# Attention inside a four-layer kernel: where VectorE makes its weight factors, when the last weight loads are asked for, and where the biases are added

## The chip, the cores and the metric

The kernel runs on one core of one Trainium2 chip. The time is device time in microseconds from launch to end, given as the median over runs. A profiled execution is a separate one; its span runs from its first to its last instruction.

## The reference, cut to what matters

Four layers run one after the other, each with a residual: `x = x + ffn(cond(x))`, with x of 8 x 128 tokens by 512. The change lies in the attention of the third layer and at the seam to what follows it:

```python
q = rope(rmsnorm(x @ Wq.T))          # 32 heads of 128
k = rope(rmsnorm(x @ Wk.T))          # 8 heads
v = x @ Wv.T
kc, vc = k_cache[block_table], v_cache[block_table]      # 512 cached rows for each of 8 sequences
scores = q @ concat(kc, k).T * SCALE                     # 640 keys, cached ones beyond the length hidden
probs = softmax(scores)
o = probs @ concat(vc, v)
y = o @ Wo.T
# next, the feed-forward of the same layer:
x = x + (y @ W.T + b) + delta(y)
```

All arithmetic is in float32.

## The kernel before

**Steps.** Attention is cut into 32 steps: `steps[n] = (qd, p)`, with `qd` one of 8 head groups (one key head and its four query heads) and `p` one of 4 pairs of sequences, so n = 4 qd + p. Within a step everything is done for both sequences j = 0, 1 of the pair.

**Seven products instead of eight.** The projection (`project`) and the output product (`leave`) multiply 2x2 block matrices with seven block products (`seven`, line 954). That needs sums of blocks on both sides. On the weight side they are the four *factors* (`blocks`, lines 866 to 879): `t1 = b12 - b11`, `t2 = b22 - t1`, `t3 = b22 - b12`, `t4 = b21 - t2`, each one VectorE subtraction, written `q_s<-q` or `q_s<-q,q_s` in the profile for the projection (128x768) and `o_s` for the output (128x512). `factors()` is a Python generator: every `next` issues one of them, so they can be placed one by one. `some(ops, k)` returns a function that issues the next k, `every(ops)` issues all that are left. On the token side the four sums are `xs` or `xs_all` (`tokens(n)`, for group 0, once for groups 1 to 6 together (for steps 4 to 7), and again for group 7) and `os` (`outputs`).

A `seven` runs on TensorE in the order one, six (t2), five (t1), six (t3), one, five (b22), six (t4). The arguments `at` name points between these at which other work is issued: `"u2"` after the second addition of the running sums `u`, `"c22"` after the additions that read the third product, and so on. The additions after a product (`put`, line 1017) write q, k and the new rows of `vals`. The last product (t4) is added into the same PSUM bank that the additions of c22 read, so TensorE can't start it before they are done.

**A step, in the order of the program.** `weigh(n, 0)`: scores of the first sequence on TensorE (`st`), exponentials on ScalarE (`pT`). `added(n, 0)`: four VectorE additions over the five blocks of keys (`part`), the first of which needs two blocks of `pT`, the second two more. `divided(n - 1)`: the previous step's `av` times the reciprocal sums `R`, two VectorE products into `oT`. `outputs(n - 1)`: the four token-side sums of `oT`. `project(n + 1)`. `rotate`, then, where a new head group begins at n + 2, the three loads of its weights (`weights`), and the POOL gathers of cached keys (`kn`). `leave(n - 1)`, whose last running sums POOL adds to y (lines 1218 and 1223). `turn` and `fetch` send queries and keys through DRAM to transpose them. Then `weigh(n, 1)` with `mix(n, 0)` (`av`) inside, `added(n, 1)`, `summed(n, 0)` and `summed(n, 1)` (a transpose `partT` and a reduction `rows`), `inverted(n)`, `mix(n, 1)`, `turn_cached(n + 2)` (two transposes `kt<-kn`, which need the gathered rows), and `tokens(n + 2)`.

**The way of the sums.** `inverted` copies the rows of three partition groups on ScalarE (line 1168), reduces, inverts and transposes on VectorE (`inv`, lines 1170 to 1172), and sends 4 KB to DRAM (`sums<-inv`, line 1175) and back to all partitions (`R<-sums`, 512 KB, line 1176). Both are on SP's queue, and the second waits there for the first.

**Order.** Nearly all of this is issued through `kept`, which keeps the order of the program on each engine's queue. Each engine works through its queue in order and waits on semaphores. What follows attention (`ending`) is partly left to a planner: its matmuls `h`, for one, have no fixed place.

**What the change moves.** In the kernel before, a new group's four projection factors are issued as follows, with n = 2, 6, ..., 26: two in step n between `added(n, 1)` and `summed(n, 1)`, one in step n + 1 after the first addition of `added`, one at `"u2"` of the next projection. The output factors of group 0 are issued in step 1: three at `"c22"` of `project`, one at `"c22"` of `leave`. `load_w2` and `load_aw` (lines 1757 to 1763) ask SP's queue for two weights of 1 MB each, `WT` and `AwT`, in step 30 before `mix`. `shifted` (line 1797) adds the biases of the feed-forward to x with four ScalarE activations, in step 31 after `weigh(31, 1)`.

Of the kernel before, what the change touches and what calls it, by code (L numbers as in the profile page):

```python
# [791 lines left out]
def attention(tc, a, x, ident, lens, kvrow, part, ww, wop, ypool, sums, rot, eps, psa, c2, chunks, mm):  # L792
# [52 lines left out]
    steps = [(qd, p) for qd in range(NQ) for p in range(NP)]  # L845
# [11 lines left out]
    def kept(i):  # L857
        return tc.keep_in_program_order(i) if running or i.ins.engine == pool.engine else i
# [38 lines left out]
    def every(ops):  # L897
        for _ in ops:
            pass
# [246 lines left out]
    def added(n, j):  # L1146

        t, u = (wk.tile([P, REP * P], F32, tag=f"part{k}{j * (k == 0)}", name=f"part{k}_{n}_{j}", bufs=1) for k in range(2))
        c = [S[n]["pT", j][:, k, :, :].rearrange("p i t -> p (i t)") for k in range(NC)]
        S[n]["part", j] = t  # L1150
        for o, l, r in ((t, c[0], c[1]), (u, c[2], c[3]), (t, t, u), (t, t, c[4])):
            kept(dve.tensor_tensor(o, l, r, ALU.add))  # L1152
            yield
# [8 lines left out]
        kept(dve.transpose(t, s["part", j].rearrange("p (b d) -> p b d", d=32)))  # L1162
        kept(dve.tensor_reduce(s["rows"][:, 0, j, :], t, AX.X, ALU.add))  # L1163

    def inverted(n):
        rows = S[n]["rows"].rearrange("p g j b -> p g (j b)")
        for g in range(1, 4):
            kept(act.copy(rows[0:32, g, :], rows[32 * g : 32 * g + 32, 0, :]))  # L1168
        r = wk.tile([32, 2, 32], F32, tag="inv", name=f"inv_{n}", bufs=1)
        kept(dve.tensor_reduce(r[:, 0, :], rows[0:32].rearrange("p g c -> p c g"), AX.X, ALU.add))  # L1170
        kept(dve.reciprocal(r[:, 0, :], r[:, 0, :]))
        kept(dve.transpose(r[:, 1, :], r[:, 0, :]))
        S[n]["R"] = R = wk.tile([P, 2, REP, P], F32, tag="R", name=f"R_{n}", bufs=1)
        here = sums[2 * n : 2 * n + 2, :].rearrange("j c -> (j c)")
        kept(sp.dma_start(here.rearrange("(c a) -> c a", a=32), r[:, 1, :]))
        kept(sp.dma_start(R.rearrange("p j i t -> p (j i t)"), here.partition_broadcast(P)))
# [102 lines left out]
    def run(pool_, end_of, bank, keep):  # L1279
        late.append(pool_)  # L1280
        y2 = ypool.tile([P, NB, D], F32, tag="y", name="y2")
        Y.append(y2)
        pool.memset(y2, 0.0)

        idle = psa.tile([P, 512], F32, tag="mm", name="idle_q", bufs=3)
        for _ in range(3):
            kept(pe.matmul(idle, x[:, 0, 0:P], x[:, 0, 0:512], start=True, stop=True))
        for j in range(2):
            squares(1, "q", j, range(REP))
            squares(1, "k", j, (0,))  # L1290
        keys_terms = rotate(1)
        read_cached = turn_cached(1, "xs")
        keys_terms()
        gather(1, "v")
        roots(1)
        rotated(1)
        normed(1)
        turn(1)
        end, prepared = None, iter(())
        w_ops, wo_ops = iter(()), WO[0].factors()  # L1300

        def some(ops, k=1):
            return lambda: [next(ops, None) for _ in range(k)]

        for n, (qd, p) in enumerate(steps):

            after = n + 1 if 0 < n < len(steps) - 1 else None
            weigh(n, 0)
            sums_of, outs = added(n, 0), iter(())
            next(sums_of)  # L1310
            some(w_ops)()
            every(sums_of)
            if n:
                divided(n - 1)
                outs = outputs(n - 1)
                if not after:
                    every(outs)
            if after:
                project(after, {
                    "u2": lambda: (every(outs), every(w_ops)),  # L1320
                    "c22": lambda: (turn_cached(2)() if n == 1 else None, some(wo_ops, 3)()),
                    "c11": lambda: (squares(after, "k", 0, (0,)), squares(after, "q", 0, (0, 1))),
                    "c12": lambda: squares(after, "q", 0, (2, 3)),
                })
                keys_terms = rotate(after)
                if n + 2 < len(steps):
                    if steps[n + 2][1] == 0:
                        weights(steps[n + 2][0])
                    gather(n + 2, "k")
                leave(n - 1, {  # L1330
                    "one": lambda: (
                        squares(after, "q", 1, range(REP)), squares(after, "k", 1, (0,)), roots(after),
                    ),
                    "c22": lambda: (every(wo_ops), keys_terms(), rotated(after), normed(after), turn(after)),
                })
                fetch(after)
                gather(after, "v")
            if n + 2 == len(steps):
                end.load_w2()
                end.load_aw()  # L1340
            mixed = mix(n, 0)
            left = (lambda: leave(n - 1),) if n and not after else ()
            weigh(n, 1, {2: (some(mixed), *left), 3: (some(mixed),), 4: (some(mixed, NC),)})
            if left:
                end.shifted()
            sums_of = added(n, 1)
            next(sums_of)
            summed(n, 0)
            if n == 0:
                next(sums_of)  # L1350
                fetch(1, read_cached)
                gather(2, "k")
            every(sums_of)
            if 0 < n < len(steps) - 2 and steps[n + 2][1] == 0:
                w_ops = W[steps[n + 2][0]].factors()
                some(w_ops, 2)()
            summed(n, 1)
            inverted(n)
            if n == 0:
                every(tokens(2))  # L1360
            if n == 5:
                prepared = end.prepare(bank, lambda shape, name: wk.tile(shape, F32, tag="xs", name=name, bufs=1))
            next(prepared, None)
            every(mix(n, 1))
            next(prepared, None)
            if n and p == 0:
                out_weights(qd)
                wo_ops = WO[qd].factors()
            if 0 < n < len(steps) - 2:
                turn_cached(n + 2)()  # L1370
                every(tokens(n + 2))
            if n == 3:
                kept(keep())
            if n == 4:
                end = end_of(kept)

            if qd == NQ - 1 and p:
                for j in range(2):
                    end.turn(y2, 2 * (p - 1) + j, bank)
            if n + 2 == len(steps):  # L1380
                end.low(0, bank)
                end.anchors(0, bank)
        divided(n)
        every(outputs(n))
        end.product(0, "st", bank)
        leave(n)
        return y2, end
# [903 lines left out]
```

## Time and profile before

| what | value |
|---|---|
| median of 3 runs | 1513.34 us (1511.30 to 1516.49) |
| the profiled execution | 1513.29 us, of which its span 1511.4 us |
| mean granted TensorE clock | 0.998 |
| busy: PE / VectorE (DVE) / ScalarE (ACT) / POOL | 1483.4 / 1079.4 / 565.6 / 847.7 us |
| matmuls st (L1132, cached and new keys) / av (L1183) | 301.5 / 290.6 us |
| DMA | 174.05 MB, mean 115 GB/s |

The page lists busy time of each engine and the costliest groups of instructions. The view of waits says, for each engine, whom it waited for: total, number, and longest. The timeline lists one engine's instructions: start, duration, engine, line, operation, output and inputs, count, and in brackets the idle time before it with the one that ended it. The chain of waits goes back from the last instruction to what released each step; "issue" is time in which an engine waited for nothing that the profile shows. Attention's steps lie between 328 and 1372 us of the span.

### The profile page before, as it was taken

Reading aid. Unit: us, or ns where it says so; the run is one execution under the profiler, and the core shown is the slowest. Engines: PE = TensorE matmul, PEld = TensorE weight load, DVE = VectorE, ACT = ScalarE, POOL = GpSimd, SP = SyncE. Lnnn points to the kernel's source line nnn. Section 1 sums busy time; section 2 is a strip of 40 time slices with the busy share of each in tenths; the row PEclk is TensorE's granted clock in tenths of the full one; section 3 lists DMA queues with packets and bytes.
Section 4 is the critical chain, followed back from the end, with each engine's and each line's share of the span. In section 5 each row is a group of like instructions: output and inputs, shape, how many; then the busy total and the mean of one; then the engine's idle time right before and its main releaser. Section 6 shows DMA issues by size and latency. Waiting matters only on the chain.

```text
span 1511.4 us, 18134 instructions
## 1 busy us (share of the span) xinstructions
PE 1483.4 (98%) x5615; PEld 939.9 (62%) x5615; DVE 1079.4 (71%) x2121; ACT 565.6 (37%) x1432; POOL 847.7 (56%) x869
## 2 busy tenths in 40 slices
PE   8999999999999999999999999999999999999998
PEld 7888787445555655555555555555555555559886
DVE  4566524388888787887778778778877888855375
ACT  1111101054444544454554444455445445431110
POOL 2232103476776777776677767677777767621210
PEclk9999999999999999999999999999999999999999
DMA  7411001144556434554444455445445544432001
GB/s 238 117 43 32 1 1 54 52 117 134 160 140 204 142 114 129 154 159 147 134 148 116 132 147 175 127 133 152 127 128 161 159 117 135 116 106 96 1 7 53
DMA packets 159306, 174.05 MB, mean 115 GB/s; under 512 B 54753, under 2 KB 129697, under 8 KB 159073
## 3 DMA queue, kind: packets, MB, share of 16 engines
q1 hardware_dynamic: 140768, 135.47, 30.8%
q0 software_dynamic: 17056, 36.49, 7.8%
q10 hardware_dynamic: 1376, 0.85, 0.2%
q8 instruction: 47, 0.77, 0.2%
q14 instruction: 59, 0.48, 0.1%
HBM read 130.66 MB, written 42.07 MB: 114 GB/s over the span
## 4 chain that ended last, share of the span: by engine, by line
PE 78%; DVE 12%; DMA 5%; issue 2%; ACT 1%; POOL 0%; SPq 0%; DVEq 0%; ACTq 0%
PE st L1132 14%; PE av L1183 13%; PE g L362 8%; PE q_six L968 7%; PE wo_two L968 5%; PE dn L362 5%; PE q_one L968 4%; PE q_five L968 4%; PE wo_one L968 3%; PE wo_six L968 3%; PE eo_l L53 2%; DVE q_s L875 2%; PE h L1719 2%; PE z L1719 2%; DMA R<-sums 2%
## 5 line engine op out<-in xcount | busy, mean ns | idle before, releaser
L911 POOL DMA_INDIRECT kn<-in_k_cache,kvrow_k x256 | 273.9, 1070 | 73.3 <-issue 69.8
L911 POOL DMA_INDIRECT vals<-in_v_cache,kvrow_v x256 | 272.7, 1065 | 73.5 <-issue 50.5
L1183 PE MATMUL av<-pT,vals 128*128 128x512 f32 x640 | 290.6, 592 | 1.5 <-DVE oT L1193 1.5
L1136 ACT ACTIVATE pT<-st,hide 128x512 f32<-128x512 f32 x256 | 176.0, 687 | 167.5 <-PE st L1132 167.2
L1132 PE MATMUL st<-qT,kT 128*128 128x512 f32 x512 | 236.1, 594 | 2.0 <-DMA qT<-turned_new 1.9
L1183 PEld LDWEIGHTS av<-pT,vals 128*128 128x128 f32 x640 | 121.4, 190 | 154.4 <-issue 147.3
L1057 POOL TENSOR_TENSOR vq<-q,txq 128x256 f32<-128x256 f32 x128 | 120.0, 966 | 150.5 <-DVE q L1017 78.5
L1132 PEld LDWEIGHTS st<-qT,kT 128*128 128x128 f32 x512 | 96.3, 190 | 111.8 <-issue 105.6
L1152 DVE TENSOR_TENSOR part<-pT 128x512 f32<-128x512 f32 x128 | 88.0, 688 | 71.8 <-ACT pT L1136 68.5
L968 PE MATMUL q_one<-q,x 128*128 128x384 f32 x256 | 93.0, 486 | 0.0
L1041 ACT ACTIVATE sqq<-q 128x128 f32<-128x128 f32 x256 | 79.4, 310 | 20.8 <-DVE q L1017 14.2
L968 PEld LDWEIGHTS q_one<-q,x 128*128 128x128 f32 x256 | 48.5, 190 | 39.8 <-issue 13.6
L968 PE MATMUL q_six<-q_s,xs_all 128*128 128x384 f32 x192 | 69.8, 486 | 0.0
L1022 ACT COPY q<-q_one 128x256 f32<-128x256 f32 x32 | 11.9, 373 | 148.7 <-PE q_one L968 148.7
L968 PE MATMUL wo_one<-o,oT 128*128 128x256 f32 x256 | 65.8, 379 | 0.2 <-DVE oT L1193 0.2
L1132 PE MATMUL st<-qT,kTn 128*128 128x512 f32 x128 | 65.4, 592 | 0.0
L1168 ACT COPY rows<-rows 32x32 f32<-32x32 f32 x96 | 20.7, 216 | 115.5 <-DVE rows L1163 114.7
L968 PE MATMUL wo_two<-o_s,os 128*128 128x256 f32 x256 | 60.6, 380 | 0.4 <-DVE vals L1017 0.4
L1136 ACT ACTIVATE pT<-st,rs 128x512 f32<-128x512 f32 x64 | 44.0, 687 | 38.4 <-PE st L1132 38.4
L429 POOL TENSOR_TENSOR ws<-wu 128x256 f32<-128x256 f32 (+1 forms) x9 | 6.6, 734 | 92.1 <-DMA wu<-in_WuT 92.1
L968 PEld LDWEIGHTS wo_one<-o,oT 128*128 128x128 f32 x256 | 48.6, 190 | 13.8 <-issue 0.5
L968 PE MATMUL q_six<-q_s,x 128*128 128x384 f32 x128 | 47.2, 492 | 9.1 <-DVE vals L1017 9.1
(451 smaller groups left out, 2861.2 us busy)
## 6 DMA issues: line engine op xcount, KB each, us to landing
turned_new<-qkt SPq DMA_DIRECT2D x126, 160.0 KB
turned_cached<-kt SPq DMA_DIRECT2D x128, 128.0 KB
kT<-turned_cached SPq DMA_DIRECT2D x32, 512.0 KB
qT<-turned_new SPq DMA_DIRECT2D x32, 512.0 KB
R<-sums SPq DMA_DIRECT2D x32, 512.0 KB
q<-in_WqT SPq DMA_DIRECT2D x8, 1024.0 KB
o<-in_WoT SPq DMA_DIRECT2D x8, 1024.0 KB
kn<-in_k_cache,kvrow_k POOLq DMA_INDIRECT x256, 3.0
```

The source lines that it names most:

```text
L53: pe.matmul(o, lhsT, rhs, start=start, stop=stop)
L362: pe.matmul(o, lhsT, rhs, start=start, stop=stop, skip_group_check=True)
L875: kept(dve.tensor_tensor(o, l, r, ALU.subtract))
L911: kept(pool.indirect_dma_start(out=d[:, c, :], out_offset=None, in_=kc if what == "k" else vc, in_offset=bass.IndirectOffsetOnAxis(ap=kvro ...
L968: kept(pe.matmul(o, l[:, c, :], r[:, c, :], start=start and c == 0, stop=c == 1, skip_group_check=True))
L1041: kept(act.activation(sq, S[n][m][:, j, i, :], AF.Square, accum_out=S[n]["ssq"][:, j, col : col + 1]))
L1057: kept(pool.tensor_tensor(to, t[:, b, :, hi : hi + 64], wx[:, b, lo : lo + 64].unsqueeze(2).to_broadcast(list(to.shape)), ALU.mult,))
L1132: kept(pe.matmul(ps, s["kT"][:, c, 4 * j : 4 * j + 4, :] if c < 4 else s["kn"][:, j], s["qT"][:, :, REP * j : REP * (j + 1), :].rearrange( ...
L1136: kept(act.activation(pT[:, c, :, :].rearrange("p i t -> p (i t)"), ps, AF.Exp, **(dict(bias=hide[:, b, c : c + 1]) if c < 4 else dict(bia ...
L1152: kept(dve.tensor_tensor(o, l, r, ALU.add))
L1183: kept(pe.matmul(ps, v[:, c, :], pT[:, c, :, :].rearrange("p i t -> p (i t)"), start=c == 0, stop=c == NC - 1, skip_group_check=True,))
L1719: return pe.matmul(o, lhsT, rhs, start=start, stop=stop, skip_group_check=True)
```

## The change

It has four parts.

1. A new group's projection factors: the first is issued inside `inverted`, behind ScalarE's row copies and ahead of VectorE's reduction of them; the second after `turn_cached(n + 2)`; the third after the first addition of the next step, as before; the fourth after the last of these additions, ahead of `divided`.
2. The output factors of group 0, in step 1: two ahead of the first addition of `added(1, 0)`, one after it, one at `"c22"` of the projection.
3. `load_w2` and `load_aw`, in step 30, follow `inverted`, so they stand behind `sums` and `R` on SP's queue.
4. `shifted`, in step 31, follows `inverted`, so the four activations stand behind the row copies on ScalarE's queue.

No instruction is added or removed.

```diff
@@ -1162,10 +1162,11 @@
         kept(dve.transpose(t, s["part", j].rearrange("p (b d) -> p b d", d=32)))
         kept(dve.tensor_reduce(s["rows"][:, 0, j, :], t, AX.X, ALU.add))
 
-    def inverted(n):
+    def inverted(n, meanwhile):
         rows = S[n]["rows"].rearrange("p g j b -> p g (j b)")
         for g in range(1, 4):
             kept(act.copy(rows[0:32, g, :], rows[32 * g : 32 * g + 32, 0, :]))
+        meanwhile()
         r = wk.tile([32, 2, 32], F32, tag="inv", name=f"inv_{n}", bufs=1)
         kept(dve.tensor_reduce(r[:, 0, :], rows[0:32].rearrange("p g c -> p c g"), AX.X, ALU.add))
         kept(dve.reciprocal(r[:, 0, :], r[:, 0, :]))
@@ -1307,9 +1308,12 @@
             after = n + 1 if 0 < n < len(steps) - 1 else None
             weigh(n, 0)
             sums_of, outs = added(n, 0), iter(())
+            if n == 1:
+                some(wo_ops, 2)()
             next(sums_of)
-            some(w_ops)()
+            (some(wo_ops) if n == 1 else some(w_ops))()
             every(sums_of)
+            every(w_ops)
             if n:
                 divided(n - 1)
                 outs = outputs(n - 1)
@@ -1317,7 +1321,7 @@
                     every(outs)
             if after:
                 project(after, {
-                    "u2": lambda: (every(outs), every(w_ops)),
+                    "u2": lambda: every(outs),
                     "c22": lambda: (turn_cached(2)() if n == 1 else None, some(wo_ops, 3)()),
                     "c11": lambda: (squares(after, "k", 0, (0,)), squares(after, "q", 0, (0, 1))),
                     "c12": lambda: squares(after, "q", 0, (2, 3)),
@@ -1335,14 +1339,9 @@
                 })
                 fetch(after)
                 gather(after, "v")
-            if n + 2 == len(steps):
-                end.load_w2()
-                end.load_aw()
             mixed = mix(n, 0)
             left = (lambda: leave(n - 1),) if n and not after else ()
             weigh(n, 1, {2: (some(mixed), *left), 3: (some(mixed),), 4: (some(mixed, NC),)})
-            if left:
-                end.shifted()
             sums_of = added(n, 1)
             next(sums_of)
             summed(n, 0)
@@ -1351,11 +1350,15 @@
                 fetch(1, read_cached)
                 gather(2, "k")
             every(sums_of)
+            summed(n, 1)
             if 0 < n < len(steps) - 2 and steps[n + 2][1] == 0:
                 w_ops = W[steps[n + 2][0]].factors()
-                some(w_ops, 2)()
-            summed(n, 1)
-            inverted(n)
+            inverted(n, some(w_ops))
+            if n + 2 == len(steps):
+                end.load_w2()
+                end.load_aw()
+            if left:
+                end.shifted()
             if n == 0:
                 every(tokens(2))
             if n == 5:
@@ -1368,6 +1371,7 @@
                 wo_ops = WO[qd].factors()
             if 0 < n < len(steps) - 2:
                 turn_cached(n + 2)()
+                some(w_ops)()
                 every(tokens(n + 2))
             if n == 3:
                 kept(keep())
```

## The prediction

> **What bounds the kernel now.** I read the page's table of engines first, then PE's waits, then PE's timeline around the largest of them, then the chain of waits back from it.
>
> ```profile
> PE 1483.4 (98%) x5615; PEld 939.9 (62%) x5615; DVE 1079.4 (71%) x2121; ACT 565.6 (37%) x1432; POOL 847.7 (56%) x869
> ```
>
> PE works nearly all the time, and the change adds and removes no matmul. It can move the end only through PE's waits. The two that matter:
>
> ```profile
> PE q_six L968 <- DVE vals L1017: 9.1, 7, 1.3
> ...
> PE av L1183 <- DVE oT L1193: 1.5, 1, 1.5
> ```
>
> Columns: total us, times, longest. Seven waits: as many as head groups with new weights. PE's timeline shows the first (start, us):
>
> ```profile
> 420.62 1.45 PE L968 MATMUL q_one<-q,x 128*128 128x384 f32 x4
> 422.16 1.56 PE L968 MATMUL q_five<-q,xs_all 128*128 128x384 f32 x4
> 425.02 1.56 PE L968 MATMUL q_six<-q_s,x 128*128 128x384 f32 x4 [1.30 <-DVE vals L1017]
> 426.41 1.03 PE L968 MATMUL wo_one<-o,oT 128*128 128x256 f32 x4
> ```
>
> Pieces of an undisturbed projection start 1.29 apart, and its wo_one starts 9.03 after its first q_one (383.22 to 392.25 one step earlier). Here q_one was at 415.46, so wo_one should start at 424.49; it starts 1.92 later. The bracket is less than the loss, since the modelled ends overlap and q_five slips as well. From wo_two to wo_two an undisturbed step takes 32.24 us (591.89 to 624.13). The seven steps with a wait take 1.93, 1.63, 1.74, 1.57, 1.70, 1.79 and 1.66 longer: **12.0 us** in all, the most that the weight factors can give.
>
> Why VectorE is late there: the chain of waits into the second of them.
>
> ```profile
> 538.71 0.96 DVE q_s L875
> ...
> 539.70 2.71 DVE q_s L875
> ...
> 545.48 2.12 DMA sums<-inv
> ...
> 547.62 4.19 DMA R<-sums
> ...
> 555.78 0.87 DVE q_s L875
> ...
> 557.23 1.56 PE q_six L968 x4
> ```
>
> Two factors stand ahead of the sums whose reciprocals (R) go through DRAM; R lands late, `divided` waits 1.40 for it, and one more factor stands between `outputs` and the additions that free q_six. The second factor takes 2.71 where its fellows take 0.95, because POOL is adding to y:
>
> ```profile
> 539.62 1.28 POOL L1223 TENSOR_TENSOR y<-y,uo 128x512 f32<-128x512 f32 x1
> 540.84 0.73 POOL L1218 TENSOR_TENSOR y<-uo,y 128x256 f32<-128x256 f32 x1
> ```
>
> In a step without factors VectorE has holes where the change puts them (last part: idle before, releaser):
>
> ```profile
> 574.87 0.37 DVE L1170 TENSOR_REDUCE inv<-rows 32x32 f32<-32x128 f32 x1 [0.74 <-ACT rows L1168]
> ...
> 580.18 0.69 DVE L1152 TENSOR_TENSOR part<-pT 128x512 f32<-128x512 f32 x1 [2.38 <-ACT pT L1136]
> 581.90 0.69 DVE L1152 TENSOR_TENSOR part<-pT 128x512 f32<-128x512 f32 x1 [1.03 <-ACT pT L1136]
> ```
>
> **What the Trainium skill says.** "SBUF — State Buffer", section "Who interferes with whom": a VectorE instruction with two SBUF inputs contends with a GpSimd one that reads SBUF, whichever issues first blocks the other for its whole length, and tensor_reduce never contends. The trace agrees: 2.71 against 0.95, and the reduction of rows at 573.45, beside the y additions at 573.50, takes its usual 0.69. "DMA: Bandwidth & Descriptors", section "Anatomy of one DMA — SWDGE (gpsimd) path": some 2 us fixed for each DMA. `sums` with 4 KB, from SP's queue, takes 2.12: agrees. Same page, "Issuing engines are not separate DMA queues": all DMAs share 16 engines. Below, a `sums` behind 2 MB takes 10.26.
>
> **The change, part by part.** I replay VectorE's queue with the spacings of the trace, PE's position up to q_one unchanged.
>
> *Weight factors, five changes without tokens* (steps 6, 10, 14, 18, 22; clock of step 6). The last addition starts 538.10. As in other steps, partT follows 0.73 later and the reduction another 0.74: 539.57 to 540.26. ACT's copies run to 540.95. The first factor, now beside them, is held by the y additions as before's second one was, so it ends at 542.4 as that did: its cover is real only up to 540.95, the rest (1.45) is paid, and counted. The chain inv takes 1.0: 543.4, against 545.45. R: 2.12 + 4.19 later, 549.8. kt: 543.56 to 544.79, if the kn rows are there: their last issue ends at 539.61, landing takes 3.1 in the median, so 542.7. Second factor: to 545.66, ahead of the first addition, which waits for pT until 546.30 anyway: hidden, 0.64 to spare. Third factor 546.90 to 547.85, in the hole before 548.02: hidden. Additions to 550.15. Fourth factor to 551.02, ahead of `divided`: R is there 1.2 earlier, so no wait replaces it. divided 551.02, u1 552.22, u2 552.88, outputs 553.35, c22's two additions 554.82 and 555.16. PE follows the start of the second by 0.34: 555.50. PE wants it at 547.96 + 7.74 = 555.70. Slack 0.2: **the whole loss goes**, 1.63 + 1.74 + 1.57 + 1.70 + 1.79 = 8.4 us.
>
> *The two changes with tokens* (steps 2, 26) have four more additions, 1.47, before the first of part. Step 2: first factor ends 410.17, kt 411.34, second factor 412.57, tokens 413.44, additions from 414.91, third factor inside, fourth 418.50, divided 419.37, u2 421.22, c22's second 423.49, PE 423.83, wanted 423.20. So 0.63 (with issue 0.74) of 1.92 stays. Step 26 likewise: PE 1210.31 instead of 1211.50. Gain 1.2 each: 2.4 us. No hole hides a factor here; the gain is the shortened chain.
>
> *Step 1, output factors.* Three of them (0.65 + 0.69 + 0.68) stand at c22 behind two transposes and hold c12's additions; wo_two waits 0.36, its step takes 0.52 longer than 32.24. Now two lie in the hole of 1.73 before part at 348.44, one in that of 1.02 before 350.16, one stays: 0.5 us gained.
>
> *Last loads, step 30.* SP's queue now has sums and R ahead of the two 1 MB loads:
>
> ```profile
> 1327.73 0.51 SPq L1763 DMA_DIRECT2D AwT<-in_AwT  x1
> 1328.29 0.88 SPq L1175 DMA_DIRECT2D sums<-inv  x1
> 1338.56 0.34 SPq L1176 DMA_DIRECT2D R<-sums  x1
> ```
>
> sums lands about 1330, R 1334. `divided` then starts when the additions end, 1340.70, not 1341.96: PE's av starts 1.26 earlier, and 0.4 stays of a wait that costs 1.63 (1341.08 expected, 1342.71 seen). The loads are asked for about 3.5 later, behind R's wait for sums, and with the 10.3 seen land by about 1341; their first user, h, starts at 1360.03: hidden. Nothing else queues on SP until 1359.06. Gain 1.3 us.
>
> *Biases, step 31.* Four activations (4.26) stand ahead of the three row copies: inv waits 1.76 instead of 0.74. Without them R is 1.0 earlier; PE fills that time with h and waits only 0.20, and 0.2 more before wo_two: gain 0.3. Behind the biases now stands the y2T copy at 1360.23, delayed 1.1 to about 1361.3; PE has h blocks to go on with: nothing, at worst 1.
>
> POOL gets no instruction and its queue keeps its order. Sum: 8.4 + 2.4 + 0.5 + 1.3 + 0.3 = **12.9 us**. The profiled execution took 1513.29 (span 1511.4 and 1.9 around it), 0.05 under the median of the runs shown: 1513.3 - 12.9 = 1500.4.
>
> Not shown by the trace: whether kn has landed when kt asks 2.06 earlier. From above: before's kt did not wait, so at most 2.06 late. Then the five save about 0.6 each and the two lose 0.87 each: a gain of 3.0 - 1.7 + 2.1 = 3.4 in all. From below: no wait, as worked out. Landing takes at most 4.8 in the window of steps 2 and 3, where 3.4 to 4 is needed; I take no wait and keep the other end.
>
> **Rivals.**
> *A, the forecast*, 0.68: 10 to 14.5 us gone; its own range is 1498.5 to 1503.5.
> *B, the wait comes back smaller*, 0.17. The slack of the five is 0.2. With VectorE 1 us later than replayed (kn, or a longer hold by POOL) the five lose 0.8 each and the two 1.0: gain 12.9 - 6.0 = 6.9, 1506.4.
> *C, no difference*, 0.10. Either kn is at its upper bound (gain 3.4, 1509.9), or the ending is laid out anew by the planner, since its matmuls are not kept in order, and PE there waits as long as three products take. A row of 42 h takes 4.85, a product has 32: 3.7 each, 11.1 in all, 1511.5. For: a wait on qT's DMA of 0.2 exists already. Against: VectorE is the releaser in all seven waits. That the change doesn't do what it says belongs here: the cover of the row copies is indeed partly empty.
> *D, slower*, 0.05. Three factors now lie beside POOL's value gathers (0.94 to 1.22 each in step 7) where one did. If each gather held a factor for h as the y additions do, q_six would start 3h - 0.8 (the hidden spare) later than replayed in the five, 3h in the two; against now that is 5(3h - 2.53) + 2(3h - 1.19), less 2.1 from the other edits: 21h - 17.1. It decides from h = 0.8; with 1.2 the loss is 8.1 us, 1521.4. Against: the one factor that lies beside a gather now (547.43, gather 547.28) takes 0.95, so h is near 0.
>
> **How the numbers follow.** The time is that of A, 1500.4. The range takes in all stalls gone (14.5: 1498.8) with run scatter below, and B and part of C above: 1497 to 1508. About 0.3%, 4.5 us, is what a measurement of this kernel can tell from no change; faster takes A and B, 0.85, the same C, 0.10, slower D, 0.05.
>
> **What would show it.** PE's waits: q_six on vals down from seven to two, each about 0.5, total near 1 us; steps 3, 7, 11, ... back to 32.24; av on oT about 0.2 to 0.4. VectorE: the factor behind the last row reduction 2.1 to 2.4 long, the others 0.95; `oT` without waits on R except in step 31; `sums` in step 30 about 2 us. Wrong would be: kt waiting on kn, factors of 1.8 beside gathers, q_five waiting on u2, or new PE waits after 1360.

## The result and the profile after

The changed kernel took **1498.14 us** in the median (1495.56 to 1500.24, 4 runs) against 1514.42 us of the kernel before (1511.30 to 1516.49, 4 runs): ratio 0.9893, 95% interval 0.9869 to 0.9918. A second comparison, described below, gave 1502.78 against 1513.64: ratio 0.9910, 0.9890 to 0.9929. So the gain is 16.3 us in one and 10.9 in the medians of the other (13.6 by its ratio); the 12.9 that the prediction added up lies inside both intervals (12.4 to 19.8 and 10.7 to 16.7 us), and its 1500.4 between the two medians. That nearness is in part luck, since the medians lie 4.6 us apart and the first gain is larger than the 14.5 that the prediction gave for all stalls gone. What can be judged is where the time went.

The profiled execution took 1495.56 us, its span 1493.8 (clock 0.999). That is 17.6 us less span than before. 4.55 of them are not the change's: the first `st` of attention starts at 324.01 instead of 328.56, and the code up to there is untouched (the last experiment comes back to this). From the first `st` to the end it is 1169.79 instead of 1182.84, **13.05 us less**.

The table of engines of the changed kernel; as many instructions on each engine as before:

```profile
PE 1479.5 (99%) x5615; PEld 940.4 (63%) x5615; DVE 1069.0 (72%) x2121; ACT 565.6 (38%) x1432; POOL 848.5 (57%) x869
```

PE is busy 3.9 us less on the same matmuls. A piece next to a stall is drawn longer (q_five 1.56 before, 1.45 now), but PE's busy time also scatters by as much: it is 1483.7 in a second trace of the changed kernel (`after_again`, below), where the stalls are gone as well. VectorE is 10.4 us less busy; 7.7 of it is the longest factor of each of the seven changes of group, 2.71 before and 1.60 to 1.62 now. PE's waits (total us, times, longest):

```profile
PE st L1132 <- DMA qT<-turned_new: 1.6, 1, 1.6
...
PE wo_one L968 <- DVE oT L1194: 0.4, 1, 0.4
PE hd L53 <- issue: 0.4, 1, 0.4
...
PE wo_two L968 <- DVE os L927: 0.3, 1, 0.3
...
PE av L1184 <- DVE oT L1194: 0.2, 1, 0.2
```

The waits of q_six for `vals`, 9.1 us in seven, are gone, all seven. The wait of `av` fell from 1.5 to 0.2. New are a short one of wo_two in the last step, where that of wo_one grew from 0.2 to 0.4, and one of "issue" in front of an `hd`, that is, one for which the profile shows no releaser. PE's timeline at the place where the first of the seven was (start, duration in us):

```profile
415.18 1.45 PE L968 MATMUL q_one<-q,x 128*128 128x384 f32 x4
416.47 1.45 PE L968 MATMUL q_five<-q,xs_all 128*128 128x384 f32 x4
417.76 1.45 PE L968 MATMUL q_six<-q_s,x 128*128 128x384 f32 x4
419.05 1.03 PE L968 MATMUL wo_one<-o,oT 128*128 128x256 f32 x4
```

Every piece is 1.29 behind the one before it. This is a change *with* tokens (step 2; the token-side sums stand in VectorE's queue there as well), where 0.6 to 0.7 us of stall had been expected to stay.

VectorE's timeline in the change of step 6, the one that the prediction replayed:

```profile
530.74 0.69 DVE L1152 TENSOR_TENSOR part<-part,pT 128x512 f32<-128x512 f32 x1
531.46 0.71 DVE L1162 STREAM_TRANSPOSE partT<-part 128x512 f32<-128x512 f32 x1
532.21 0.69 DVE L1163 TENSOR_REDUCE rows<-partT 128x16 f32<-128x512 f32 x1
532.81 1.61 DVE L875 TENSOR_TENSOR q_s<-q 128x768 f32<-128x768 f32 x1
534.35 0.35 DVE L1171 TENSOR_REDUCE inv<-rows 32x32 f32<-32x128 f32 x1
...
536.71 0.92 DVE L875 TENSOR_TENSOR q_s<-q,q_s 128x768 f32<-128x768 f32 x1
538.99 0.69 DVE L1152 TENSOR_TENSOR part<-pT 128x512 f32<-128x512 f32 x1 [1.37 <-ACT pT L1136]
539.60 0.95 DVE L875 TENSOR_TENSOR q_s<-q 128x768 f32<-128x768 f32 x1
540.71 0.69 DVE L1152 TENSOR_TENSOR part<-pT 128x512 f32<-128x512 f32 x1 [0.15 <-issue]
```

Three factors lie where they were dealt. The second leaves 1.37 us of the hole unused, the third fills nearly all of the next (0.15 left). `inv` starts 3.61 after the last addition (530.74); in the kernel before it was 6.38:

```profile
538.10 0.69 DVE L1152 TENSOR_TENSOR part<-part,pT 128x512 f32<-128x512 f32 x1
544.48 0.36 DVE L1170 TENSOR_REDUCE inv<-rows 32x32 f32<-32x128 f32 x1 [0.74 <-ACT rows L1168]
```

And the first factor takes 1.61, not the 2.71 of the second one in the kernel before, which stood through both of POOL's additions. POOL at the same moment:

```profile
532.26 1.28 POOL L1224 TENSOR_TENSOR y<-y,uo 128x512 f32<-128x512 f32 x1
533.49 1.52 POOL L1219 TENSOR_TENSOR y<-uo,y 128x256 f32<-128x256 f32 x1
```

A factor is "asked for" where it starts in the timeline, and "held" where it then takes longer than its usual 0.95. This one was asked for 0.55 after the start of the first addition. By the lengths it was let in when that one ended (533.54; 0.95 later is 534.49, and it ended at 534.42), and this time the second addition was held: 1.52 instead of 0.73.

**Where the 13.05 us came from**, by the intervals from wo_two to wo_two in both traces (before, after; an undisturbed one has 32.24):

| interval | before | after | gain | predicted |
|---|---|---|---|---|
| five changes without tokens, over 32.24 each | 8.42 | 0.04 | 8.38 | 8.4 |
| two changes with tokens, over 32.24 each | 3.60 | 0.00 | 3.60 | 2.4 |
| first `st` to the first wo_two (output factors, step 1) | 31.95 | 31.43 | 0.52 | 0.5 |
| to the wo_two of step 31 (last loads) | 33.19 | 33.08 | 0.11 | 1.3 |
| from there to the end (biases) | 166.86 | 166.60 | 0.26 | 0.3 |
| the other 22 intervals | | | 0.18 | |
| sum | | | 13.05 | 12.9 |

The five terms of the prediction come to 12.87, as predicted, but two of them are off by 1.2 us each, in opposite directions. The experiments ask what is behind the first two rows, and why those two terms were wrong. The last row hides one more: from the first wo_two to the second it takes 32.60 before and 32.24 after, and the rest scatters against that. It is no chance. The interval is 32.52 to 32.88 in all eight traces with the output factors in their old place, and 32.24 in five of the six with them moved (32.39 in the sixth).

### The profile page after: what moved, and what is told of

Read it like the earlier page. It is cut to its first block, busy times and chain, and to the rows that moved or that the text cites. A ratio compares the mean times of both kernels' runs of the same rounds, so it can differ in the third digit from the quotient of the medians.

```text
span 1493.8 us, 18138 instructions
## 1 busy us (share of the span) xinstructions
PE 1479.5 (99%) x5615; PEld 940.4 (63%) x5615; DVE 1069.0 (72%) x2121; ACT 565.6 (38%) x1432; POOL 848.5 (57%) x869
## 4 chain that ended last, share of the span: by engine, by line
PE 94%; DVE 3%; issue 1%; DMA 1%; ACT 0%; POOL 0%; SPq 0%; DVEq 0%; ACTq 0%
PE st L1132 18%; PE av L1184 18%; PE q_six L968 8%; PE g L362 8%; PE wo_two L968 6%; PE q_one L968 5%; PE q_five L968 5%; PE dn L362 5%; PE wo_six L968 4%; PE wo_one L968 4%; PE eo_l L53 3%; PE h L1723 2%; PE z L1723 2%; PE o L1723 1%; PE midp_l L53 1%; PE gu L362 1%
## 5 line engine op out<-in xcount | busy, mean ns | idle before, releaser
L911 POOL DMA_INDIRECT vals<-in_v_cache,kvrow_v x256 | 269.7, 1053 | 73.5 <-issue 61.3
L362 PE MATMUL g<-xs,ws 128*128 128x256 f32 (+1 forms) x240 | 55.1, 379 | 0.0
```

Of the source, the lines that this page charges most:

```text
L362: pe.matmul(o, lhsT, rhs, start=start, stop=stop, skip_group_check=True)
L911: kept(pool.indirect_dma_start(out=d[:, c, :], out_offset=None, in_=kc if what == "k" else vc, in_offset=bass.IndirectOffsetOnAxis(ap=kvro ...
```

## The experiments

Single profiled executions scatter by several us at places that no edit touches. So mechanisms are read from intervals and waits of the traces, and times from kernels that were run several times beside each other on one chip.

### The projection factors alone, and the rest alone

`factors_only` is the kernel before with part 1 of the change:

```diff
-                    "u2": lambda: (every(outs), every(w_ops)),
+                    "u2": lambda: every(outs),
...
+            summed(n, 1)
             if 0 < n < len(steps) - 2 and steps[n + 2][1] == 0:
                 w_ops = W[steps[n + 2][0]].factors()
-                some(w_ops, 2)()
-            summed(n, 1)
-            inverted(n)
+            inverted(n, some(w_ops))
...
                 turn_cached(n + 2)()
+                some(w_ops)()
```

and `every(w_ops)` behind the last addition of `added(n, 0)`. `rest_only` has parts 2 to 4 and leaves the projection factors where they were.

> The kernel before with the four projection factors dealt out as in the change (first inside inverted, second after turn_cached, fourth ahead of divided); the output factors of group 0, the last loads and the biases stay in their old places. Theory (the factors are nearly all of the gain): the seven steps that follow a new group's factors fall from 33.8-34.2 us to 32.24 from wo_two to wo_two, 12.0 us in all, so the ratio is about 0.992; the wait of wo_two in step 1 (0.4) and of av in step 31 (1.5) stay. Rival (the other three edits carry much of the measured 16 us): at most 8 us, ratio above 0.995.

> The changed kernel with the projection factors back in their old places; the output factors, the loads and the biases stay moved. Theory: the seven waits of q_six stay, 9.1 us by the view of waits; step 1 is 0.5 shorter, step 31's av waits 0.2 instead of 1.5, but the step before it is longer by 1.2; 0.9 us gained in all, ratio 0.999 to 1.000. Rival: 4 us or more are gained, ratio 0.997 or less.

Measured: `factors_only` 1497.53 against 1513.20, ratio 0.9895 (0.9878 to 0.9912); all seven waits gone, 12.06 us less from the first `st` to the end, first interval (first `st` to first wo_two) 31.95, step 31's interval 33.20 with the `av` wait of 1.5 still there. `rest_only` 1511.50 against the same, ratio 0.9986 (0.9976 to 0.9996): 2.1 us faster, 0.6 to 3.6. Its seven changes take 33.9 to 34.2 as before, and step 31's interval fell to 31.91, 1.28 less. Its first interval is 33.12 and not 31.4, since the first row of eight `st` takes 5.37 there (3.67 in the kernel before); so its trace, from the first `st` to the end, is no shorter than before's.

So the projection factors carry the gain. By the times they gain 15.9 us (13.3 to 18.5), more than the 12.06 of the trace and than the ratio of 0.992 that had been expected; where the excess lies is not shown. The 2.1 of the three small edits agree with the prediction's 0.5 + 1.3 + 0.3, but the interval is too wide to confirm them. And the 1.28 of the last loads, plain in the trace here, is missing from that of the changed kernel (0.11); more on that below.

### Which of the four factors it is

`pair_only` moves the first and the second factor (behind the row copies, and behind `turn_cached`) and leaves the fourth at `"u2"`. `fourth_only` moves the fourth alone:

```diff
             every(sums_of)
+            every(w_ops)
...
-                    "u2": lambda: (every(outs), every(w_ops)),
+                    "u2": lambda: every(outs),
```

> The kernel before, with only the first two factors moved (one inside inverted, one after turn_cached); the fourth stays behind outputs, right ahead of the additions that free q_six. Theory (the pair is late because it stands ahead of the sums, and the place of the fourth factor does not matter): all seven steps at 32.24, no wait of q_six on vals, about 12 us less. Rival (the factor right ahead of the additions is what TensorE waits for): 0.3 to 0.9 us of wait stays in each of the seven.

> The kernel before, with only the fourth factor moved ahead of divided; the first two stay ahead of the sums. Theory: in the five changes without tokens it fills part of divided's wait for R (1.3 to 1.4 us) and q_six starts 0.87 earlier; in the two with tokens VectorE's queue is full and nothing is gained. The five steps lose 0.7 to 0.9 instead of 1.6 to 1.8, the two still 1.9 and 1.7; 4.4 us gained in all. Rival (the factor right ahead of the additions is what TensorE waits for): at least 0.87 in all seven, 6 us or more.

Measured: `pair_only` 1499.15 (one run), 11.68 us less from the first `st` to the end, all seven waits gone. `fourth_only` 1513.62 (one run). Its line in PE's waits, where the kernel before has 9.1 in seven with 1.3 at most:

```profile
PE q_six L968 <- DVE vals L1017: 3.1, 7, 0.4
```

The five changes without tokens take 32.97 to 33.22, about 0.9 us less than before in each; the two with tokens nothing less (34.59 and 33.91). From the first `st` to the end it is 1182.46, only 0.4 less than before: from step 31's wo_two to the end, which no edit touches, it took 1.7 us longer in this execution, and step 31's interval 0.8. By its time, too, it is no faster than the kernel before.

What follows: the place of the fourth factor is not what matters; with the other two moved it may stay. Alone it gains where `divided` waits for R: it then lies inside that wait and no longer between `outputs` and the additions that free q_six. In a change with tokens the trace of the kernel before has no such wait to put it in. What carries the gain is that two factors went out of the way of the sums, and R comes while it is not yet wanted.

### Must the first factor stand behind the row copies?

`pair_split` moves the pair by less: the first factor stays ahead of `summed(n, 1)`, the second stands inside it, between its transpose and its reduction. All else is the kernel before.

```diff
-                some(w_ops, 2)()
-            summed(n, 1)
+                some(w_ops)()
+                summed(n, 1, some(w_ops))
...
```

> The kernel before, with the second of the two early factors issued between partT and the reduction rows of summed(n, 1), 0.7 us later, in the middle of POOL's first addition to y instead of right at its start. Theory (a factor that asks in the middle of the first addition gets in between the two, as in the changed kernel; one that asks at its very start is held through both): the factor takes 1.5 us, POOL's second addition 1.5 instead of 0.72, the sums go out 1.2 us earlier and the seven steps lose 0.2 to 0.8 us instead of 1.6 to 1.9: about 9 us gained. Rival (it is held through both whenever it asks): the factor takes 2.0 to 2.1 us, POOL's second addition 0.72, about 4.5 us gained.

Measured: 1503.63 (one run). The seven changes lose 1.38, 0.90, 0.36, 0.53, 0.49, 0.20 and 0.87: 4.7 in all, so 7.3 us gained, between the 9 and the 4.5 that had been expected. `inv` starts 5.64 after the last addition, between 6.38 (12.0 lost) and 3.61 (0.04 lost): the loss follows the delay of the sums. VectorE and POOL in the change of step 6:

```profile
535.24 2.21 DVE L875 TENSOR_TENSOR q_s<-q,q_s 128x768 f32<-128x768 f32 x1
```

```profile
534.65 1.29 POOL L1224 TENSOR_TENSOR y<-y,uo 128x512 f32<-128x512 f32 x1
535.88 0.74 POOL L1219 TENSOR_TENSOR y<-uo,y 128x256 f32<-128x256 f32 x1
```

The second factor was asked for 0.59 after POOL's start, practically as in the changed kernel (0.55), and yet both additions went ahead of it (2.21, and 0.74 for POOL's second). So it is not the moment of asking that let the first factor of the changed kernel in.

### What lets a factor in between POOL's two additions

Two things differed between those two places: the instruction ahead of the factor (a reduction there, a transpose here) and its form (`q_s<-q` there, `q_s<-q,q_s` here, which reads what the factor before it wrote). `mid_transpose` is the changed kernel with the first factor behind a transpose (issued twice, so that the moment stays):

```diff
         kept(dve.transpose(t, s["part", j].rearrange("p (b d) -> p b d", d=32)))
+        if between:
+            kept(dve.transpose(t, s["part", j].rearrange("p (b d) -> p b d", d=32)))
+            between()
         kept(dve.tensor_reduce(s["rows"][:, 0, j, :], t, AX.X, ALU.add))
...
+                summed(n, 1, some(w_ops))
...
-            inverted(n, some(w_ops))
+            inverted(n, lambda: None)
```

`mid_reduce` is the split kernel with a reduction ahead of its second factor:

```diff
                 some(w_ops)()
-                summed(n, 1, some(w_ops))
+                part = S[n]["part", 1].rearrange("p (b d) -> p b d", d=32)
+                kept(dve.tensor_reduce(S[n]["rows"][:, 0, 1, :], part, AX.X, ALU.add))
+                some(w_ops)()
+            summed(n, 1)
```

> The kernel after, but in the seven changes of group the transpose partT of the second sequence is issued twice and the first factor follows the second of them, ahead of the row reduction. So the first factor is again asked for some 0.6 us after the start of POOL's first y addition, as in the changed kernel (0.55) and in the split kernel (0.59), but now behind a transpose. Theory 'the instruction ahead decides' (a reduction ahead lets the factor in between POOL's two additions, a transpose does not): factor 2.0 to 2.2 us, POOL's second addition 0.72 to 0.74. Rival 'the form decides' (q_s<-q gets in, q_s<-q,q_s, which reads the factor just made, does not): factor 1.5 to 1.7 us, POOL's second addition 1.5. If the lengths differ among the seven: a race of moments, neither. Time: one more transpose and the reduction behind the factor, 1.6 + 0.7 us later sums: up to 2 us lost in each change, 1500 to 1512.

> The split kernel, but between its first and its second factor stands a row reduction of part (its output is written again by the true one) instead of the transpose, and the transpose follows the second factor. The second factor (q_s<-q,q_s) is asked for about 0.6 us after the start of POOL's first y addition, behind a reduction. Theory 'the instruction ahead decides': it gets in between, 1.5 to 1.7 us, POOL's second addition 1.5. Rival 'the form decides': 2.0 to 2.2 us, POOL's second addition 0.72 to 0.74. Time: one reduction (0.7) more on the way of the sums than the split kernel (1503.6): 1503 to 1511.

Measured: in `mid_transpose` the factor is let in, in six of seven changes alike (1.56 to 1.58, POOL's second addition 1.50); in the seventh it asks 0.14 into the second addition and waits for its end. In `mid_reduce` the second factor is held through both in six of six (2.23 to 2.24, POOL's second 0.73). VectorE and POOL of `mid_transpose`, then of `mid_reduce`, in step 6:

```profile
536.20 1.58 DVE L875 TENSOR_TENSOR q_s<-q 128x768 f32<-128x768 f32 x1
```

```profile
535.62 1.28 POOL L1227 TENSOR_TENSOR y<-y,uo 128x512 f32<-128x512 f32 x1
536.85 1.50 POOL L1222 TENSOR_TENSOR y<-uo,y 128x256 f32<-128x256 f32 x1
```

```profile
537.26 2.23 DVE L875 TENSOR_TENSOR q_s<-q,q_s 128x768 f32<-128x768 f32 x1
```

```profile
536.70 1.29 POOL L1223 TENSOR_TENSOR y<-y,uo 128x512 f32<-128x512 f32 x1
537.93 0.73 POOL L1218 TENSOR_TENSOR y<-uo,y 128x256 f32<-128x256 f32 x1
```

"The instruction ahead decides" is refuted by both. "The form decides" fits these, but not the seventh change of `mid_reduce`, where POOL comes earlier: VectorE, then POOL, in step 26.

```profile
1189.29 0.69 DVE L1152 TENSOR_TENSOR part<-part,pT 128x512 f32<-128x512 f32 x1
1189.89 2.90 DVE L875 TENSOR_TENSOR q_s<-q 128x768 f32<-128x768 f32 x1
```

```profile
1190.02 1.28 POOL L1223 TENSOR_TENSOR y<-y,uo 128x512 f32<-128x512 f32 x1
1191.24 0.73 POOL L1218 TENSOR_TENSOR y<-uo,y 128x256 f32<-128x256 f32 x1
```

Here a `q_s<-q` is held through both (2.90). But it is the only such case, and this factor asked 0.13 ahead of POOL, the others behind it; so it doesn't refute "the form decides" for a factor that asks while POOL adds.

One reading covers all seven changes in all fourteen traces: what counts is the VectorE instruction that ended just as POOL's first addition started. In 43 of the 98 changes it is one with two inputs, and POOL starts within 0.05 us of its end, as if it had taken over from it (`part` above ends at 1189.98 and POOL starts at 1190.02). In 42 of these the factor is held through both additions; in the other, the seventh of `mid_transpose`, it asks too late to tell. In the remaining 55 it is a transpose, which ended 0.08 to 0.10 ahead of POOL's start, and the factor gets in between every time. That reading was formed from these traces and not tried by itself, and the form goes with it in all cases but one; which of the two decides stays open.

The two kernels also measure the spare of the replay. `mid_transpose` delays `inv` to 5.02 after the last addition, 1.41 later than the changed kernel. Its five changes without tokens still lose nothing, and its two with tokens lose 1.41 and 1.34, nearly all of it: those two had no spare left. `mid_reduce` is back at 6.38 and at 12.9 us lost; its time is 1511.96, that of `mid_transpose` 1502.31 (one run each).

### The last loads

`loads_early` is the changed kernel with `load_w2` and `load_aw` back ahead of `mix`; `loads_late` asks for them one step later and on ScalarE's queue. `after_again` is the changed kernel once more.

```diff
@@ loads_early
+            if n + 2 == len(steps):
+                end.load_w2()
+                end.load_aw()
             mixed = mix(n, 0)
@@ loads_late
             weigh(n, 0)
+            if n + 1 == len(steps):
+                end.load_w2()
+                end.load_aw()
...
-        kept(sp.dma_start(W["2"], chunks(a["W2T"])))
+        kept(act.dma_start(W["2"], chunks(a["W2T"])))
```

> The changed kernel once more, for a narrower ratio and a second trace. Theory (what lies between the first st and the end got 13.1 us shorter in the first trace, 1.2 of a further gain was lost to 66 small matmuls z and hd that ran 1.2 late in that one execution, and the opening, which the change does not touch, was 4.6 shorter by chance): z and hd take 3.7 from the first z to the next st, not 4.9; step 31 takes 31.9 us; first st to end is 1168.5 to 1169; the first st starts anywhere from 323.8 to 329. Rival (the moved loads delay z and hd, and the opening is shorter in every execution of this kernel): z and hd take 4.9 again, step 31 takes 33.1, first st at 324.0.

> The changed kernel with the two loads back ahead of mix in step 30, so ahead of sums on SP's queue. Theory (the loads hold sums, sums holds R, R holds divided): sums takes about 10 us instead of 1.4 to 2.7, av waits 1.5 for oT, step 31 takes 33.2 us again, 1.3 us more than without. Rival (R is hidden either way): step 31 takes 31.9.

> The changed kernel with the two 1 MB loads on ScalarE's DMA queue, behind the exponentials of weigh(31, 0), so that neither R nor z and hd run beside them. Theory (chance): step 31 takes 31.9 us as in the changed kernel run again, no difference in time beyond 0.3 us. Rival (the loads delay z and hd): only here step 31 falls to 31.9, and this kernel is 1.2 us faster than the changed one.

Measured: `after_again` 1502.78 against 1513.64, ratio 0.9910 (0.9890 to 0.9929); `loads_late` 1497.51, ratio 0.9883 (0.9864 to 0.9903); `loads_early` 1499.60 (one run). The intervals just overlap; none of these versions can be told from the changed kernel.

In `after_again` the seven changes take 32.24 each, as in the first trace. Nearly all else that had been expected of it was missed: from the first `st` to the end it is 1177.4, not 1168.5 to 1169, and step 31 takes 34.77, not 31.9. In `loads_late` step 31 takes 34.56, so the 31.9 that either theory had for it did not come.

SP's queue in step 30 of the changed kernel, then of `loads_early`:

```profile
1310.72 0.33 SPq L1176 DMA_DIRECT2D sums<-inv  x1
1313.40 0.34 SPq L1177 DMA_DIRECT2D R<-sums  x1
1313.79 0.43 SPq L1763 DMA_DIRECT2D WT<-in_W2T  x1
```

```profile
1313.39 0.51 SPq L1767 DMA_DIRECT2D AwT<-in_AwT  x1
1313.95 0.81 SPq L1176 DMA_DIRECT2D sums<-inv  x1
1323.67 0.34 SPq L1177 DMA_DIRECT2D R<-sums  x1
```

R can be asked for 2.7 us after `sums` where the loads stand behind, 9.7 where they stand ahead. So far it is as predicted. Yet `loads_early` has no wait for it: its `av` waits 0.2, and its interval of step 31 is 32.98, against 33.08 in the changed kernel. What hides the late R shows in PE's timeline, ahead of the second sequence's scores. First `rest_only`, then the changed kernel:

```profile
1331.42 1.06 PE L1722 MATMUL z<-y2T,A 128*32 128x128 f32 x26
1332.41 1.12 PE L53 MATMUL hd<-WH,y2T 128*128 128x16 f32 x8
```

```profile
1314.94 1.40 PE L1723 MATMUL z<-y2T,A 128*32 128x128 f32 x26
1316.28 0.66 PE L53 MATMUL hd<-WH,y2T 128*128 128x16 f32 x2
1317.35 0.87 PE L53 MATMUL hd<-WH,y2T 128*128 128x16 f32 x6 [0.42 <-issue]
```

The small matmuls (32 z and 16 hd; the 66 of the expectations is a miscount) break off and go on about 1.2 us later: from the first z to the next `st` it takes 3.75 in one kernel and 4.93 in the other. In some traces the row of eight `st` behind them is longer too. The changed kernel, then `after_again`:

```profile
1318.07 3.68 PE L1132 MATMUL st<-qT,kT 128*128 128x512 f32 x8
```

```profile
1323.37 5.03 PE L1132 MATMUL st<-qT,kT 128*128 128x512 f32 x8
```

These two delays account for step 31. `rest_only`, with neither, takes 31.91. Add what the break takes beyond 3.75 and the row beyond 3.68, and the intervals of eight of the nine traces with a break come out to about 0.01 (the changed kernel 33.08, `loads_early` 32.98, `after_again` 34.77, `loads_late` 34.56). PE comes to its `av` by that much later, and finds R there, also in the four of them with early loads. The ninth, `pair_split`, has early loads and a break (4.74), and `av` still waits 0.9; its R was asked for 10.2 after `sums`. So the break and the wait for R share one slack, and where there is a break the place of the loads gains little or nothing. Since the break appears with the loads at their old place (`loads_early`, 4.83) and on another queue (`loads_late`, 4.76), they are not its cause.

### Does the break go with the kernel?

Two kernels without the break were run again, unchanged.

> The kernel before once more, for what scatters between executions. Theory 'the late small matmuls go with the kernel': the 66 matmuls z and hd of step 30 run without a break again (z x26 in 1.06 us, hd x8 in 1.11 twice). Rival 'they go with the execution': a break of 1.1 to 1.3 us may appear. Opening: first st at 326 to 329 us if it goes with the kernel, 324 to 329 if with the execution. Steps 3, 7, ..., 27 again 33.8 to 34.2 us. Time 1511 to 1516.

> The kernel with the projection factors moved alone once more. Theory 'the late small matmuls go with the kernel': z and hd of step 30 without a break. Rival 'with the execution': a break of 1.1 to 1.3 us is as likely as in the five traces that had it out of ten. Opening: first st at about 323.8 us if it goes with the kernel, anywhere from 324 to 329 if with the execution. None of the seven waits. Time 1495 to 1501.

Measured: 1514.84 and 1499.98 (one run each). Both have the break now: `before_again` 4.80 from the first z to `st`,

```profile
1333.11 0.53 PE L53 MATMUL hd<-WH,y2T 128*128 128x16 f32 x3
1334.34 0.83 PE L53 MATMUL hd<-WH,y2T 128*128 128x16 f32 x5 [0.70 <-issue]
```

and `factors_again` 4.87. So it does not go with the kernel. Sorted by chip, it is all or none: `factors_only`, `rest_only`, `pair_only` and `fourth_only` shared a chip and have none (3.75 or 3.76 in each); the four with `after_again` (`pair_split` among them) shared another and all have it; so do the four with `before_again` on a third. Of the two traces that are compared here, before's has none and the changed kernel's has it. Whether it goes with the chip or with the moment can't be told, and what it is stays open: the traces show no releaser, and the last fetch of instructions ahead of it, an obvious candidate, starts 7.9 to 8.0 us before the first z in all fourteen, with the break or without.

The opening goes the same way: first `st` at 324.39 in `before_again`, 328.56 in the trace of before, the same code. PE then waits 2.1 for `tgm` and 1.1 for the weight `wg`; `before_again` has neither of them. So the 4.55 us of the profiled pair are scatter. Six of the seven changes take 33.85 to 34.18 in `before_again`, as expected; the seventh takes 36.43, where q_five waits 2.0 for VectorE.

In step 1, `before_again`, `factors_again` and `mid_reduce` wait 1.3 for wo_two, where the kernel before waited 0.36; their first intervals are 33.45 to 33.96. `mid_transpose`, on the same chip but with the output factors moved, has no such wait and takes 31.43.

## Why the prediction was right, and which of its steps were not

**What bounds the kernel: right.** What the edits gained is time that PE lost at its waits. PE's share of the chain that ends last rose from 78% to 94%.

**The five changes: right, 8.4 and 8.38.** No wait took the place of the one removed. `kt` did not wait for `kn` (0.17 of issue ahead of it), so the open bound fell on the side that was taken. `divided` waits for R in step 31 alone, as said. The slack was larger than worked out: 0.2, plus the 0.7 of the shorter hold, would leave the changed kernel 0.9; by `mid_transpose` it has at least 1.4. So the replay put these five at least 0.5 too late, which did no harm.

**The two changes with tokens: mis-sized, 2.4 predicted, 3.60 measured.** The step that failed is "the first factor, now beside them, is held by the y additions as before's second one was". It was held through one addition (1.61), not through both (2.7), so `inv` came 0.7 us sooner than replayed, just what the two were to keep losing. In the five that only added to the spare. That the two came out just without a loss is luck. The Trainium skill, "SBUF — State Buffer", section "Who interferes with whom", was read as if a run of POOL additions held VectorE to its end; the traces agree that one addition holds it (1.61 instead of 0.95), and show both answers for two in a row.

**Step 1: right in kind, too small.** 0.5 was predicted and the first interval gained 0.52, but the 0.36 behind the first wo_two was left out; together 0.9, and over 2, by single executions, on the chip where wo_two waited 1.3.

**The last loads: shown in one trace, given back in this one.** 1.3 was predicted, 1.28 measured in `rest_only`, 0.11 here. The step that failed is that `av` would start earlier by all that `divided` did: PE itself came 1.2 us later, by the break.

**The biases: 0.3 predicted, 0.26 in this pair, but not by that way.** The last wo_two comes sooner (22.15 to 21.28 from the one before), since the planner now puts 32 h in the row ahead of it instead of 42; the ten h are made up afterwards, and the tail grows from 144.71 to 145.32. Over all traces the two together take 166.6 to 168.7 with the biases moved (six) and 166.4 to 168.5 with them in place (eight). A gain of 0.3 can't be seen in that, and is not shown.

**The rivals.** B (the wait comes back smaller) needed VectorE to be late by 1 us; it was early. C fell: `kt` waited for no `kn` in the seven changes, and the ending's new layout (32 h instead of 42) stays within the scatter. D (factors held by the value gathers) fell: the factor at 539.60 lies across two gathers and takes 0.95.

**What should have shown it.** That q_six would keep two waits of 0.5, and that the factor behind the reduction would take 2.1 to 2.4, was wrong (none, 1.61). Of the signs of being wrong, a new wait in the last step came, but small (wo_two, 0.26). That the others take 0.95, that the steps return to 32.24 and that `av` waits 0.2 to 0.4 was right.

## What to carry to other kernels

Where one engine's late product stalls the bound engine, follow its chain back to the transfer it waits for, and look at what stands ahead of that transfer's start. Two cheap instructions moved from there into holes that they fit took away 12 us of stalls; moving the one nearest to the stalled matmul took away some 4. Two delays that meet at the same wait are not added: a fix of one can be worth nothing in an execution in which the other is there. And a sum that comes out right can hide two wrong terms, so check it interval by interval.

## What the hardware showed unexpectedly

- A weight factor that VectorE asks for while POOL adds (0.95 alone) is held through one addition (1.6) or through both of two in a row (2.2), with the same moment of asking (0.54 to 0.59 after POOL's start); at one place of one kernel it was the same way in all changes, save in two changes where POOL came earlier. Where it is let in, POOL's second addition pays instead: 1.5 instead of 0.73.
- 48 small matmuls in a row (z and hd) take 3.75 us in five traces and 4.74 to 5.27 in nine, all or none on each of three chips, with no releaser in the profile.
- A row of eight `st` matmuls takes 3.68 us, or 5.0 to 5.3 in five of the nine traces with such a break, with no releaser either.
